# Cross-attention and expert kernel: the first loads and weight turns reordered, the mask spread by a product

## The chip, the cores and the metric

The kernel runs on one core of one Trainium2 chip, as one launch. The metric is device time in microseconds (us) of one execution; lower is better. A core has TensorE (PE: products and weight loads), VectorE (DVE), ScalarE (ACT), GpSimd (POOL) and SyncE (SP, which only issues transfers here). Each works through its own instructions in order and waits for the others by semaphores. SBUF is the on-chip memory, PSUM the memory that PE writes to.

## What is computed

Two layers on x (8 batches of 256 rows by 512 columns), each added to x after a layer norm.

1. Cross-attention. The rows of a batch (256) are channels, the 512 columns are positions. 16 heads of 16 channels:

```
q = Wq @ layernorm(x) + bq;  k = Wk @ src + bk;  v = Wv @ src + bv
mask = m[t] * m[s]
dot = mask * (q . k) / 4 - (1 - mask) * 1e6
out = (softmax(dot) * mask) @ v
x = x + out
```

2. A feed-forward layer on tokens (the 256 rows of each batch, 512 wide): a shared gated expert, a router that picks two of eight experts for each token, and the bf16 experts, weighted by the router's softmax.

The change touches only how the first batch's attention begins.

## The kernel before, in words

**Tiling.** Everything is laid out in tiles of 128 partitions. Attention works in groups of four heads: a batch has four groups (NG), the whole run 32, and `G` counts them. For each group, q and k tiles (128 x 512) hold four heads of 16 channels in blocks of 32 rows; the other 16 rows of a block carry mask and bias terms, so that one 32-row product yields the masked score. The rows come from `project_qk` (L393): a product with the turned weight (`product`, L399), then `rows` (L405), which on DVE multiplies the product by a 0/1 column (`mine`) and adds an extra tile. The extra tile is made by `extra_rows` (L380) from the mask spread over all partitions (`mb`) and the columns `alpha` and `beta`; `alpha` takes in the biases (`bias_terms`, L217).

**The loop over scores.** `row_max` (L419) computes scores of one quarter of the positions for two heads (two products into the PSUM banks s1 or s2), and DVE takes the row maximum into `nm`; eight calls make a group. `take_max` (L432) turns the maxima on PE (psn) and subtracts them from q on DVE. `exp_scores` (L441) computes the scores again the other way round, ACT takes the exponential, and `attend` (L455) multiplies with V, which `project_v` (L355) makes a quarter at a time. In the main loop (L1167 to L1244) the maxima run a group ahead of the exponentials.

**How order is set.** The order is written by hand (`manual_schedule`): program order is each engine's order. Fixed lists, such as `plan`, put the feed-forward work, the weight turns and the transfers at steps of the loop. The scheduler only adds the waits. Tiles come from pools with a number of buffers ("acc" has five, "e" three, PSUM's "mm" two); a new tile waits until the tile that many earlier is done with. Transfers of SP and ACT use eight semaphores in turn, so every ninth transfer waits until the eighth before it has landed.

**The start, which the change is about.** L126 to L136 issue the loads of batch 0: SP takes x's first half, the mask broadcast to 128 partitions (`partition_broadcast`, L128), x's second half, both halves of the context in one transfer, then Wv; ACT takes Wk, Wq and the two biases (`bflat`). `make_identity` (L139) makes `ident`. `row_terms` (L199) makes the 0/1 columns on DVE. Then come L1074 to L1103:
- `busy(n)` (L1042) issues n transposes of `ident` into a tile that nobody reads: filler on PE.
- `square` (L1049) turns a weight with four transposes (`turn_square`, L235; rows pt L239) and copies it out on ACT in four parts.
- `start_stats` (L341) takes mean and variance of half of x (DVE: st L327, mv L328, ve L330; POOL: rs L332).
- `shifted` (L1063) subtracts the mean and multiplies by the mask on DVE; `scaled` (L1070) multiplies by 1/sigma on ACT (first half), L1088 does so on DVE (second half).
- `mask_context` (L336) multiplies the context by the mask on DVE, two instructions.
- products `q_part`, `k_part` and rows `q_rows`, `k_rows` by parts.

Then eight `row_max` of group 0 (L1129 to L1141), with the turns of the shared expert's first weights between them (`weights`, pt L267), the mask columns `mcol`, and the router's load and turn (`load_router`, L248); k's rows for the second group (G = 1) come after the first maximum. `best = row_max(1, 0, 0, ...)`, `take_max(0)` and V's first quarter (L1146) follow, then the main loop.

Of the kernel before, what the change touches and what calls it, by code (L numbers as in the profile page):

```python
# [9 lines left out]
F32 = mybir.dt.float32  # L10
# [7 lines left out]
P = 128  # L18
# [8 lines left out]
NG = 4  # L27
# [9 lines left out]
def xattn_ffn_kernel(  # L37
# [85 lines left out]
        "mb": one.tile([P, T], F32, tag="mb", name="mb0"),  # L123
        "ctx": one.tile([P, 2, T], F32, tag="ctx", name="ctx0"),
    }
    nc.sync.dma_start(out=S[0]["x"][:, 0, :], in_=x[0, :P, :])  # L126
    wk_nat, wq_nat = load_square(Wk), load_square(Wq)
    nc.sync.dma_start(out=S[0]["mb"], in_=mask[0, 0].partition_broadcast(P))  # L128
    nc.sync.dma_start(out=S[0]["x"][:, 1, :], in_=x[0, P:, :])
    bflat = five.tile([2 * NG, 4, HD], F32, tag="acc", name="bflat")  # L130
    for side, bias in enumerate((bq, bk)):
        nc.scalar.dma_start(
            out=bflat[NG * side : NG * side + NG], in_=bias.rearrange("(c j d) -> c j d", j=4, d=HD)
        )
    nc.sync.dma_start(out=S[0]["ctx"], in_=src[0].rearrange("(h p) t -> p h t", p=P))
    wv_nat = load_square(Wv, nc.sync)  # L136

    ident = const.tile([P, P], F32, name="ident")
    make_identity(nc, ident)  # L139
# [77 lines left out]
    def bias_terms():  # L217

        for a in range(2):
            nc.vector.tensor_scalar(bnat[:, :, a, :], bflat, odd[: 2 * NG, a : a + 1], None, ALU.mult)  # L220
        pt = ps_m.tile([P, 2, NG // 2, 2], F32, tag="long", name="pt", bufs=1)
        nc.tensor.transpose(
            pt.rearrange("p s c a -> p (s c a)"), bnat.rearrange("r j a d -> r (j a d)"), ident[: 2 * NG, : 2 * NG]
        )
        of = lambda side: pt[:, side].rearrange("p c a -> p a c")
        nc.vector.scalar_tensor_tensor(alpha[:, 0], of(0), 0.25, terms[:, 0], ALU.mult, ALU.add)
        nc.vector.tensor_add(alpha[:, 1], of(1), terms[:, 1])

# [16 lines left out]
    sguT = wts.tile([P, 2, NKC, I + E], F32, name="sguT")  # L245
    sdT = wts.tile([P, 3, T], F32, name="sdT")

    def load_router():  # L248
        nat = five.tile([E, T], F32, tag="acc", name="wnat")
        nc.sync.dma_start(out=nat, in_=router_w)  # L250
# [90 lines left out]
    def start_stats(b, i):  # L341
        s = S[b]
        s["stats", i] = norm_stats(s["x"][:, i, :])
# [695 lines left out]
        assert not items  # L1039


    def busy(n):  # L1042

        for _ in range(n):
            nc.tensor.transpose(idle, ident, ident)

    idle = ps_av.tile([P, P], F32, tag="av", name="idle")

# [22 lines left out]
        nc.scalar.mul(s0["xm"][:, i, :], s0["xm"][:, i, :], s0["stats", i][1])  # L1071

    row_terms()
    busy(15)  # L1074
    square(wk_nat, WkT, 1.0, ps_s, "s1")
    busy(3)
    start_stats(0, 0)
    shifted(0)
    start_stats(0, 1)
    square(wq_nat, WqT, 0.25, ps_s, "s2")  # L1080
    bias_terms()
    busy(6)
    scaled(0)
    shifted(1)
    q_part, q_rows = project_qk(0, 0, True)
    k_part, k_rows = project_qk(0, 1, True)
    q_part(0)
    nc.vector.tensor_scalar(s0["xm"][:, 1, :], s0["xm"][:, 1, :], s0["stats", 1][1], None, ALU.mult)  # L1088
    extra_rows(0, 0, nc.scalar, (0,))
    mask_context(0, nc.vector)  # L1090
    busy(4)
    q_part(1)
    wv = turn_square(wv_nat, ps_s, "s2")
    extra_rows(0, 1, nc.scalar, (0,))
    q_rows(0)
    for kc in range(2):
        k_part(kc)
    k_rows(0)
    busy(8)
    nc.scalar.copy(WvT, wv)  # L1100
    extra_rows(0, 0, nc.scalar, (1,))
    extra_rows(0, 1, nc.scalar, (1,))
    q_rows(1)  # L1103
    for nm in NM:
        nc.gpsimd.memset(nm, 0.0)
    for e in range(E):
# [22 lines left out]
    for r in range(8):  # L1129
        row_max(0, r // 2, r % 2, ("s1", "s2")[r % 2])  # L1130
        if r % 2:
            weights.pop(0)[1]()
        else:
            busy(1 if r else 0)
        if r == 0:
            k_rows(1)
            pt = ps_m.tile([P, B * 4], F32, tag="long", name="pt", bufs=1)
            nc.tensor.transpose(pt, mnat, ident[: B * 4, : B * 4])
            nc.scalar.copy(mcol, pt)
        elif r == 1:  # L1140
            load_router()  # L1141
    best = row_max(1, 0, 0, "s1", True)
    busy(2)
    take_max(0)
    best()
    project_v(0, 0)  # L1146
    casts, turns = expert_weights()
    V_AT = [(2, 5), (2, 7), (3, 1), (3, 3)]
    blank = three.tile([P, T], BF16, tag="xnb", name="blank")
# [17 lines left out]
    for b in range(B):  # L1167
# [26 lines left out]
        for g in range(NG):  # L1194
            G = NG * b + g
            for h in range(8):
                st, half = divmod(h, 2)

                short = G == 0 and h < 6
                R = 8 * (G + 1) + h + LEAD - short  # L1200
                if (G or h) and R // 8 < last:
                    row_max(R // 8, (R % 8) // 2, R % 2)
                exp_scores(G, st, half if short else 1 - half, "s2" if R // 8 < last else ("s1", "s2")[h % 2])
                if G == 0 and h == 0:
                    row_max(1, 0, 1)
                if half == 0 and st > 0:
                    attend(G, st - 1)
                if G > 0 and h == 0:
                    attend(G - 1, NSTEP - 1)
                    divide_copy(G - 1)  # L1210
                if h == 8 - LEAD and G + 1 < last:
                    take_max(G + 1)
                if G > 0:
                    pb, pg = divmod(G - 1, NG)
                    if h == 1 + pg % 2:
                        divide(G - 1)
                    if pg % 2 == 1:

                        if b == pb == B - 1 and h == 5:
                            token_norm(pb, 0, nc.vector)  # L1220
                        elif h + (b == pb == B - 1) in FFN:
                            FFN[h + (b == pb == B - 1)](pb, pg // 2)
                if g == 0 and h == 6 and b + 1 < B:
                    load_batch(b + 1)
                if g == 1 and h == 0 and b + 1 < B:
                    mask_context(b + 1)
                if g == 1 and h in (2, 3) and b + 1 < B:
                    start_stats(b + 1, h - 2)
                if g == 1 and h == 5 and b + 1 < B:
                    start_norm(b + 1, nc.gpsimd)  # L1230
                if b == 0 and g == 0 and h in (0, 5, 7):
                    project_v(0, (0, 5, 7).index(h) + 1)
                if (g, h) in V_AT and b + 1 < B:
                    project_v(b + 1, V_AT.index((g, h)))
                if g % 2 == 1 and h == 7 and G + 3 < last:
                    extra_rows(G + 3, 0, nc.gpsimd)
                if g % 2 == 0 and h == 1 and G + 2 < last:
                    extra_rows(G + 2, 1, nc.gpsimd)
                if g % 2 == 0 and h in (1, 3) and G + 2 < last:
                    project_qk(G + 2, h // 2)  # L1240
                for go in plan[8 * g + h]:
# [88 lines left out]
```

## Time and profile before

| what | value |
|---|---|
| median of the runs | 871.96 us (870.93 to 879.49, three runs) |
| the profiled execution's own time | 873.27 us |
| its span (first to last instruction) | 871.5 us |
| mean granted clock of TensorE | 0.996 |
| busy: PE, DVE, ACT, POOL | 825.3, 581.8, 364.6, 312.2 us |
| instructions | 13399 |
| bytes moved by the transfers | 75.31 MB, 86 GB/s on average |

The profile is one execution, recorded in the same form for all engines. The page gives busy times and shares; the chain of waits is followed back from the last instruction, each step to what released it; the timeline lists instructions in order of time (start, length, engine, line, operation, out<-in, shapes, count; in brackets the idle time before and what ended it); the windows give the busy time of each engine in a stretch, with the clock granted to PE (1.00 is full speed) and the transfers' share and rate. Names such as `psq<-xm,WqT` are the program's own: the q product from the normalized x and the turned weight. One fp32 product of 512 columns shows as two records. "PEld" is PE's weight load, "SPq" and "ACTq" the issue of transfers.

### The profile page before, as it was taken

How to read it: one execution, taken by the hardware profiler on the slowest of the kernel's cores; microseconds unless marked ns; L12 is line 12 of the kernel's file. 1: busy time of each engine (PE TensorE's matmuls, PEld its weight loads, DVE VectorE, ACT ScalarE, POOL GpSimd, SP SyncE). 2: the span in 40 equal slices, each digit the busy share in tenths (PEclk: the TensorE clock that was granted, in tenths of full speed). 3: DMA queues.
4: the chain of work that ended last, by engine and by line, in shares of the span. 5: the costliest groups of instructions: out<-in, count | busy, mean ns of one | idle time of the engine just before them, and what ended most of it. 6: DMA issues, size and time to landing. Idle time of an engine off the chain costs nothing.

```text
span 871.5 us, 13399 instructions
## 1 busy us (share of the span) xinstructions
PE 825.3 (95%) x4978; PEld 341.4 (39%) x4990; DVE 581.8 (67%) x1105; ACT 364.6 (42%) x475; POOL 312.2 (36%) x380
## 2 busy tenths in 40 slices
PE   7988989999999999999999999999999999899997
PEld 5322333333333334333434333433343333455573
DVE  5766767775777676867786768676776674543347
ACT  3234444443444344433444343434343445356632
POOL 3114303542354345343625151605251223155520
PEclk8999999999999999999999999999999999999999
DMA  5116963221561157114712350001000000267646
GB/s 153 58 39 214 342 213 77 34 42 43 125 104 23 36 126 129 22 38 113 125 34 42 87 102 1 25 21 65 1 25 13 13 13 25 61 146 171 148 151 258
DMA packets 92099, 75.31 MB, mean 86 GB/s; under 512 B 60320, under 2 KB 77755, under 8 KB 91652
## 3 DMA queue, kind: packets, MB, share of 16 engines
q1 hardware_dynamic: 85428, 54.10, 23.1%
q0 software_dynamic: 5904, 19.70, 10.6%
q8 instruction: 40, 0.66, 0.4%
q10 hardware_dynamic: 704, 0.66, 0.2%
q14 instruction: 23, 0.19, 0.1%
HBM read 38.10 MB, written 40.79 MB: 91 GB/s over the span
## 4 chain that ended last, share of the span: by engine, by line
PE 70%; DVE 20%; issue 5%; POOL 2%; DMA 2%; ACT 1%; DVEq 0%; SPq 0%; POOLq 0%; ACTq 0%
PE s L425 24%; DVE nm L427 10%; PE av L463 9%; PE psy L987 5%; PE psq L400 4%; PE pu L929 3%; PE psk L400 3%; PE ey L838 2%; PE s L448 2%; DVE q L407 2%; PE eg L809 2%; PE psv L367 2%; PE eu L809 2%; PE pgu L929 2%; PE pg L929 2%
## 5 line engine op out<-in xcount | busy, mean ns | idle before, releaser
L450 ACT ACTIVATE e<-s 128x1024 f32<-128x1024 f32 x256 | 262.0, 1023 | 399.6 <-PE s L448 397.6
L427 DVE TENSOR_REDUCE nm<-s 128x2 f32<-128x1024 f32 x256 | 313.2, 1224 | 143.8 <-PE s L448 132.4
L425 PE MATMUL s<-k,q 32*128 32x512 f32 x1024 | 287.6, 640 | 26.5 <-DVE nm L427 24.4
L448 PE MATMUL s<-q,k 32*128 32x512 f32 x1024 | 288.5, 640 | 0.7 <-issue 0.7
L463 PE MATMUL av<-e,V 128*32 128x512 f32 x1024 | 137.4, 605 | 0.2 <-ACT e L450 0.2
L425 PEld LDWEIGHTS s<-k,q 32*128 32x128 f32 x1024 | 76.5, 183 | 131.8 <-DVE nm L427 108.0
L390 POOL TENSOR_SCALAR extra<-mb,alpha,beta 128x512 f32<-128x512 f32 x60 | 45.6, 764 | 147.0 <-DVE q L407 146.3
L332 POOL TENSOR_TENSOR rs<-ve,mhalf 128x1 f32<-128x1 f32 x32 | 17.9, 561 | 216.7 <-DVE ve L330 214.5
L448 PEld LDWEIGHTS s<-q,k 32*128 32x128 f32 x1024 | 76.5, 182 | 4.7 <-issue 4.3
L463 PEld LDWEIGHTS av<-e,V 128*32 128x32 f32 x1024 | 20.3, 108 | 98.2 <-issue 96.3
L187 POOL DMA_INDIRECT xs<-xnb,at x30 | 30.2, 1006 | 74.0 <-DVE at L658 59.3
L815 DVE SCALAR_TENSOR_TENSOR hz<-eth,eu 128x352 bf16<-128x352 f32 x45 | 23.4, 520 | 41.6 <-ACT eth L814 17.0
L987 PE MATMUL psy<-sdT,h 128*128 128x512 f32 (+1 forms) x90 | 45.3, 615 | 0.2 <-issue 0.2
L929 PE MATMUL pu<-xT,sguT 128*128 128x256 f32 x128 | 36.7, 403 | 0.0
L929 PE MATMUL pg<-xT,sguT 128*128 128x256 f32 x128 | 35.3, 401 | 0.0
L367 PE MATMUL psv<-WvT,ctx 128*128 128x256 f32 x128 | 34.7, 393 | 0.0
L929 PE MATMUL pgu<-xT,sguT 128*96 128x256 f32 (+1 forms) x128 | 34.1, 393 | 0.0
L809 PEld LDWEIGHTS <-late_ctx 128*128 128x128 bf16 x296 | 27.6, 98 | 14.0 <-issue 2.6
L400 PE MATMUL psq<-xm,WqT 128*128 128x512 f32 x64 | 33.0, 636 | 0.0
L187 POOL DMA_INDIRECT whose<-who,at x30 | 29.0, 968 | 9.1 <-issue 9.1
L407 DVE SCALAR_TENSOR_TENSOR q<-psq,mine,extra 128x512 f32<-128x512 f32 x32 | 22.6, 746 | 13.9 <-PE psq L400 13.9
L929 PEld LDWEIGHTS pu<-xT,sguT 128*128 128x128 f32 x128 | 21.8, 189 | 25.4 <-issue 23.6
(213 smaller groups left out, 987.5 us busy)
## 6 DMA issues: line engine op xcount, KB each, us to landing
xs<-blank SPq DMA_DIRECT2D x7, 1920.0 KB
ctx<-in_ctx_dram SPq DMA_DIRECT2D x8, 512.0 KB
x<-in_x_dram SPq DMA_DIRECT2D x7, 512.0 KB
accd<-acc SPq DMA_DIRECT2D x12, 256.0 KB
again<-accd POOLq DMA_DIRECT2D x12, 256.0 KB
out_dram<-again SPq DMA_DIRECT2D x12, 256.0 KB
gu<-in_L_ffn_w_gate_dram POOLq DMA_DIRECT2D x8, 352.0 KB
gu<-in_L_ffn_w_up_dram POOLq DMA_DIRECT2D x8, 352.0 KB
```

The source lines that it names most:

```text
L187: i = nc.gpsimd.indirect_dma_start(to[:, :], bass.IndirectOffsetOnAxis(ap=rows, axis=0), what, None, **bounds).ins
L367: nc.tensor.matmul(ps, ct[:, kc, sc * P : (sc + 1) * P], WvT[:, kc, :], start=(kc == 0), stop=(kc == 1))
L390: engine.tensor_scalar(t, S[b]["mb"], at, be, ALU.mult, ALU.add)
L400: nc.tensor.matmul(ps, W[:, kc, g // 2].rearrange("p j a d -> p (j a d)"), rhs[:, kc, :], start=(kc == 0), stop=(kc == 1),)
L425: nc.tensor.matmul(ps[:, jj, :], q[r, tci * P : (tci + 1) * P], k[r, :], start=True, stop=True)
L427: best = lambda: nc.vector.reduce_max(NM[G % 2][:, tci, c0 : c0 + 33 : 32], ps, axis=AX.X)
L448: nc.tensor.matmul(ps[:, jj, :], k[r, sc * P : (sc + 1) * P], q[r, :], start=True, stop=True)
L450: nc.scalar.activation(e, ps, AF.Exp)
L463: nc.tensor.matmul(AVT[G][32 * j : 32 * j + 32, :], V[:, sc, 2 * g + j // 2, j % 2 : j % 2 + 2, :].rearrange("p o d -> p (o d)"), et[j // ...
L809: nc.tensor.matmul(ps, xT[:, kc, :], weights_of(t, GU, I, (m * NKC + kc) * I), start=(kc == 0), stop=(kc == NKC - 1),)
L929: lambda kc=kc: nc.tensor.matmul(ps, sguT[:, m, kc, i0 : i0 + n + more], s["xT"][:, kc, :], start=(kc == 0), stop=(kc == NKC - 1))
L987: nc.tensor.matmul(t["y"], t["h"][:n, ic, tt * P : (tt + 1) * P], sdT[:n, ic, :], start=(ic == 0 and b < B - 1), stop=(ic == 2),)
```

## The change

Only the start and one step of the first group differ.

- Loads. SP issues x's two halves one after the other, then a single row of the mask (2 KB, into `mrow`, the rest of which a DVE memset has set to zero), then the context in two transfers, Wv and the router's weight. ACT issues the two biases first, then Wq, then Wk. `bflat`, `mrow` and the router's tile lie in the pool "e" instead of "acc".
- Mask. A constant `top` (128 x 128, ones in the first row, zero elsewhere; two memsets on DVE) is multiplied with `mrow` on PE: every partition of the product holds the mask row. ACT copies it to `mb`.
- Biases. The two multiplications of `bias_terms` go from DVE to ACT and stand first there; the turn on PE comes right after nine fillers (in place of fifteen). The DVE part is returned as `spread_out` and placed after the first statistics.
- Order. Wq is turned before Wk; first group's extra rows, the mask of the context and the second half's scaling come before the projections; Wv's turn comes after the k products instead of between the q and k products. The fillers are 9, 2, 3, 6, 2 and 5 in place of 15, 3, 6, 4 and 8.
- First maxima. k's rows of the second group come ahead of the first maximum; V's first quarter stands behind the third maximum's products instead of behind `take_max(0)`; the router is turned at r = 5 and its load has moved to the start; the fillers in that stage are two at r = 4 and r = 6 in place of one at r = 2, 4 and 6.
- Main loop. At G = 0, h = 5, three fillers (into a tile of the bank "long") follow the last maximum of group 1.

```diff
-    nc.sync.dma_start(out=S[0]["x"][:, 0, :], in_=x[0, :P, :])
-    wk_nat, wq_nat = load_square(Wk), load_square(Wq)
-    nc.sync.dma_start(out=S[0]["mb"], in_=mask[0, 0].partition_broadcast(P))
-    nc.sync.dma_start(out=S[0]["x"][:, 1, :], in_=x[0, P:, :])
-    bflat = five.tile([2 * NG, 4, HD], F32, tag="acc", name="bflat")
+    mrow = three.tile([P, T], F32, tag="e", name="mrow")
+    bflat = three.tile([2 * NG, 4, HD], F32, tag="e", name="bflat")
+    rnat = three.tile([E, T], F32, tag="e", name="rnat")
+    nc.vector.memset(mrow, 0.0)
+    top = const.tile([P, P], F32, name="top")
+    nc.vector.memset(top, 0.0)
+    nc.vector.memset(top[:1, :], 1.0)
+    for i in range(2):
+        nc.sync.dma_start(out=S[0]["x"][:, i, :], in_=x[0, i * P : i * P + P, :])
+    nc.sync.dma_start(out=mrow[:1, :], in_=mask[0])
     for side, bias in enumerate((bq, bk)):
         nc.scalar.dma_start(...)
-    nc.sync.dma_start(out=S[0]["ctx"], in_=src[0].rearrange("(h p) t -> p h t", p=P))
+    wq_nat, wk_nat = load_square(Wq), load_square(Wk)
+    for i in range(2):
+        nc.sync.dma_start(out=S[0]["ctx"][:, i, :], in_=src[0, i * P : i * P + P, :])
     wv_nat = load_square(Wv, nc.sync)
+    nc.sync.dma_start(out=rnat, in_=router_w)
...
-            nc.vector.tensor_scalar(bnat[:, :, a, :], bflat, odd[: 2 * NG, a : a + 1], None, ALU.mult)
+            nc.scalar.mul(bnat[:, :, a, :], bflat, odd[: 2 * NG, a : a + 1])
...
     row_terms()
-    busy(15)
-    square(wk_nat, WkT, 1.0, ps_s, "s1")
-    busy(3)
+    busy(9)
+    spread_out = bias_terms()
+    ps = ps_m.tile([P, T], F32, tag="mm", name="psm")
+    nc.tensor.matmul(ps, top, mrow, start=True, stop=True)
+    nc.scalar.copy(s0["mb"], ps)
     start_stats(0, 0)
+    spread_out()
     shifted(0)
+    extra_rows(0, 0, nc.scalar, (0,))
+    busy(2)
+    square(wq_nat, WqT, 0.25, ps_s, "s2")
     start_stats(0, 1)
-    square(wq_nat, WqT, 0.25, ps_s, "s2")
-    bias_terms()
-    busy(6)
     scaled(0)
     shifted(1)
+    busy(3)
+    square(wk_nat, WkT, 1.0, ps_s, "s1")
+    extra_rows(0, 1, nc.scalar, (0,))
+    busy(6)
+    nc.vector.tensor_scalar(s0["xm"][:, 1, :], s0["xm"][:, 1, :], s0["stats", 1][1], None, ALU.mult)
+    mask_context(0, nc.vector)
     q_part, q_rows = project_qk(0, 0, True)
     k_part, k_rows = project_qk(0, 1, True)
     q_part(0)
-    nc.vector.tensor_scalar(s0["xm"][:, 1, :], s0["xm"][:, 1, :], s0["stats", 1][1], None, ALU.mult)
-    extra_rows(0, 0, nc.scalar, (0,))
-    mask_context(0, nc.vector)
-    busy(4)
+    busy(2)
     q_part(1)
-    wv = turn_square(wv_nat, ps_s, "s2")
-    extra_rows(0, 1, nc.scalar, (0,))
     q_rows(0)
     for kc in range(2):
         k_part(kc)
     k_rows(0)
-    busy(8)
-    nc.scalar.copy(WvT, wv)
     extra_rows(0, 0, nc.scalar, (1,))
     extra_rows(0, 1, nc.scalar, (1,))
+    wv = turn_square(wv_nat, ps_s, "s2")
+    busy(5)
+    nc.scalar.copy(WvT, wv)
     q_rows(1)
+    k_rows(1)
...
-            busy(1 if r else 0)
+            busy(2 if r > 2 else 0)
         if r == 0:
-            k_rows(1)
...
-        elif r == 1:
-            load_router()
+        elif r == 2:
+            project_v(0, 0)
+        elif r == 5:
+            turn_router()
...
-    project_v(0, 0)
...
                 if G == 0 and h == 5:
                     row_max(1, 3, 1)
+                    busy(3, ps_m.tile([P, P], F32, tag="long", name="idle", bufs=1))
```

More of the change, by code (lines that the diff above doesn't have):

```diff
@@ L224, in bias_terms, with spread_out @@
         )
-        of = lambda side: pt[:, side].rearrange("p c a -> p a c")
-        nc.vector.scalar_tensor_tensor(alpha[:, 0], of(0), 0.25, terms[:, 0], ALU.mult, ALU.add)
-        nc.vector.tensor_add(alpha[:, 1], of(1), terms[:, 1])
+        def spread_out():
+            of = lambda side: pt[:, side].rearrange("p c a -> p a c")
+            nc.vector.scalar_tensor_tensor(alpha[:, 0], of(0), 0.25, terms[:, 0], ALU.mult, ALU.add)
+            nc.vector.tensor_add(alpha[:, 1], of(1), terms[:, 1])
+        return spread_out
     WqT = wts.tile([P, 2, 2, 4, 2, HD], F32, name="WqT")
@@ L246, in xattn_ffn_kernel, with turn_router @@
     sdT = wts.tile([P, 3, T], F32, name="sdT")
-    def load_router():
-        nat = five.tile([E, T], F32, tag="acc", name="wnat")
-        nc.sync.dma_start(out=nat, in_=router_w)
+    def turn_router():
+        nat = rnat
         pt = ps_m.tile([P, NKC, E], F32, tag="mm", name="pt")
@@ L1039, in spread, with busy @@
         assert not items
-    def busy(n):
+    def busy(n, into=None):
         for _ in range(n):
-            nc.tensor.transpose(idle, ident, ident)
+            nc.tensor.transpose(into or idle, ident, ident)
     idle = ps_av.tile([P, P], F32, tag="av", name="idle")
```

## The prediction

> **What bounds the kernel now.** I read the page's span and chain shares first, then the chain of waits over the first 34 us, then the timeline and the windows of that stretch, because the diff ends at about 53 us: all later code is word for word the same.
>
> ```profile
> span 871.5 us, 13399 instructions
> ...
> PE 70%; DVE 20%; issue 5%; POOL 2%; DMA 2%; ACT 1%; DVEq 0%; SPq 0%; POOLq 0%; ACTq 0%
> ```
>
> TensorE (PE) and VectorE (DVE) hold 90% of the chain. The steady loop hands over between them, the start does not. The chain of waits at the start (start, length, what):
>
> ```profile
> 1.64 6.84 DMA x<-in_x_dram
> 8.48 0.02 issue
> 8.51 0.71 DVE st L327
> ...
> 9.54 0.42 DVE bnat L220 x2
> 9.96 0.04 issue
> 10.00 0.27 PE pt L222
> 10.27 1.47 PE idle L1045 x6
> 11.75 1.71 PE psq L400 x2
> 13.45 0.85 PE idle L1045 x4
> 14.31 1.11 PE psq L400 x2
> 15.42 0.44 PE pt L239 x4
> 15.86 1.72 PE psk L400 x4
> 17.58 0.87 PE idle L1045 x8
> 18.45 0.04 issue
> 18.49 1.19 PE s L425 x7
> ```
>
> Until 8.48 the end is set by the load of x's second half; then by the bias turn, filler and projections on PE. The first score product starts at **18.49**. The same chain reaches the turn of the first maxima (psn) at 32.19, so the stage of eight maxima takes 13.70. Why are the projections so slow? The windows (length, busy PE, PEld, DVE, ACT, POOL, then granted clock, DMA share, GB/s) and the timeline say:
>
> ```profile
> 7.00:8.00 1.00, 0.13 (x1) 0.13 (x2) 0.75 (x1) 0.00 (x0) 0.00 (x0) 0.94 1.05 404
> 8.00:9.00 1.00, 0.99 (x4) 0.58 (x4) 0.49 (x1) 0.00 (x0) 0.00 (x0) 0.50 0.98 355
> ```
>
> ```profile
> 1.35 3.35 PE L1045 MATMUL idle<-ident 128*128 128x128 f32 x15 [1.35 <-POOL mhalf L154]
> ...
> 2.68 1.28 ACT L1056 ACT_TABLE_LOAD   x1 [2.68 <-issue]
> ...
> 7.08 0.75 DVE L1066 SCALAR_TENSOR_TENSOR xm<-x,mv,mb 128x512 f32<-128x512 f32 x1 [2.00 <-DMA mb<-in_mask_Bx1x_fk_dram]
> ```
>
> PE starved from 5.64 to 7.87, the granted clock fell to 0.50 at about 7.87 and came back between 14.6 and 14.7. One projection product costs 1.71 at half clock, 0.86 at full (psk: two in 1.72). Filler transposes cost 0.21 to 0.22 at half clock (six in 1.47), 0.11 at full (eight in 0.87). The fifteen of the opening also run at 0.22 (3.35/15): PE starts at half speed, although the windows print 1.00 there.
>
> **The change, part by part.** I build the new start on the same clock.
>
> Loads. The broadcast mask (256 KB written, landed 7.06) goes; a row of 2 KB comes. SP issues x0, x1 (0.73 to 1.6), then the mask row, which waits for a DVE memset; DVE is free from about 0.7 and POOL's 128x512 memset took 0.50, so it is done by 1.3 and holds up nothing queued behind it on SP. In before some 650 KB had landed by 4.6 (the windows' GB/s summed). x0, x1 and Wq are 768 KB, so they and the row queued behind x1 land at **about 5.0**, against 8.48 for x1. Wk and ctx follow by about 7, ahead of their use. SP's later issues: ctx1 waits for x0, Wv for a bias, the router's load moves ahead of mnat, bvb and gate rows, each at 0.34 to 0.6; all are used after 12, so they cost nothing. Gate rows and Wv no longer queue behind bflat and the router for the five "acc" buffers.
>
> Mask by product. On the path now: bias loads, table load, two bias multiplications on ACT, bias turn, product, ACT copy, all in order. Biases are issued first on ACT, at 0.7 to 1.65. Nearest row: the router's 16 KB load, issued at 19.69, released SP about 1.5 later (SP's waits). For the second bias, issued from 1.4, that gives 2.9; the Trainium skill (page DMA: Bandwidth & Descriptors, Anatomy of one DMA) puts the fixed cost of a transfer at some 2.0, which gives an estimate of 3.4. The row is the shorter and is this chip's; x's packets are in the way here: I take 3.0. The table load now waits for the biases: 3.0 to 4.3 (1.28). Multiplications: the same two took 0.42 on DVE, so 4.75; bias turn 0.27. The mask product is then ready at **5.1**, set equally by its row. It is one 128x512 product, 0.86 or 1.71.
>
> Clock. The Trainium skill (page TensorE: Matmul & The Clock Gate, Part 1) says that the throttle is lifted only after a busy window of about 3.4 us, free-running. This speaks against the change: nine fillers end at 3.35, then PE waits 1.4 for the biases. The row agrees in kind: in before, a gap of 1.02 (8.98 to 10.0) postponed the release to 14.67. By the rule the product is slow (1.71) and release comes between 8.5 and 11.9, after an unbroken 3.4 to 6.8 from 5.1; by the printed 1.00 it would be full speed throughout. I take half clock to 9.9.
> - Product 5.1 to 6.8, ACT copy (0.58, the row of WvT's copy) to **7.45**. No gain for the mask itself, which landed at 7.06.
> - DVE from there: shift 0.75, second statistics 1.10 (8.51 to 9.60), shift 0.75, scale 0.49, context mask 1.47: ends 12.0. In before it ended at 13.2, since x1 came late.
> - ACT: extra row 0.80, WqT copies 0.79 (Wq is turned by 8.1), scaled 0.74: xm's first half at 9.8.
> - PE: two fillers, Wq turn, three fillers, Wk turn, six fillers: 6.8 + 0.44 + 0.88 + 0.65 + 0.88 = 9.65; six fillers across the release, to 10.5. This is what the first q product waits for (ACT was ready at 9.8).
> - q product, two fillers, q product, two k products at full clock: 0.86 + 0.22 + 0.86 + 1.72, with 0.1 of gaps to 14.25; k rows on DVE 0.75: first score product at **15.0**, 3.5 earlier. Wv's turn and five fillers (0.99) lie beside the k rows.
> Both bounds: product at full clock at once, mask at 6.6, score at 13.4; release not before 11.9, score at 15.9.
>
> Stage of eight maxima. k of the second group moves ahead of the first maximum: +0.67 on DVE, but PE feeds that stage: two score products, the mask turn and four weight turns take 2.9 before the third score, and DVE ends the first maximum at 0.7 + 0.7 + 1.2 = 2.6. It removes the wait of the router's turn for those rows (1.35 of PE wait in before). From third score to psn, before: seven scores of 1.06, five fillers 1.15, three weight turns 1.66 = 10.2. After: 7.42 + V's first quarter 0.86 + six fillers 1.11 + 1.66 + router turn 0.25 = 11.3. So 2.9 + 11.3 = 14.2 against 13.70: **a loss of 0.5**. V left psn's other side, where its 0.86 lay beside DVE's subtraction (0.69): 0.07 saved there, and its 0.60 on DVE lay ahead of an 0.80 wait: nothing.
>
> Three fillers at the sixth step: in before PE waits 1.33 there (52.2 to 53.5) for a maximum; they take 0.33 to 0.6. If that cover were gone they would cost 0.33. The two DVE memsets for top (about 0.3) delay the mask terms, done at 3.1 while x0 lands at 3.96: cover 0.8.
>
> **Sum**: -3.5 + 0.5 = **-3.0**. The later loop is unchanged and every transfer in it is issued by program position, so the shift carries to the end. The profiled execution: 871.5 span plus 1.8 around it = 873.27; after, 868.5 span. It stands 1.3 above the median, 871.96; I carry the difference over: **869.0**.
>
> **Rivals.**
> 1. The main one: half clock through the mask product, release near 10: 869.0, own range 867.5 to 870.5. For: fillers of 0.22 in the opening. Chance 0.65.
> 2. PE at full speed from the mask product on. For: the printed 1.00, and two thirds of a busy window. Against: 0.22 per filler. Score at 13.4, saving 5.1 - 0.5 = 4.6: 867.4; with the biases and row also earlier by a microsecond, 866.2. Chance 0.15.
> 3. It doesn't do what it says: the earlier score is absorbed later, because a wait in the first batch (its buffers, loads of weights) was set by the old load times. Against: from 34 us on every piece of the chain is PE or DVE. Time 871.5 to 872.5. Chance 0.10.
> 4. Slower: the path of the biases. Everything now hangs on 1 KB loads that before had until 9.5 to land. If they or the row, sharing engines with x0 and Wq, release the mask product only at 8.1 instead of 5.1, the 3.0 are used up, and each microsecond later costs one. At 10: 873.9. For: the trace does not show when they landed. Against: 1.5 for the router. Chance 0.10.
>
> **How the numbers follow.** The likeliest is rival 1's 869.0. The range takes it, most of 2 and the near half of 3: 866.2 to 871.9, leaving 0.2 outside (deepest of 2, far half of 3, all of 4). One per cent, about what a measurement of this kernel tells from no change, is 8.7 us: no case reaches it except a mechanism I do not see in a start of 18.5 us. Faster by over 1%: 0.03; within: 0.93; slower: 0.04.
>
> **What would show it.** The first score product (18.49) near 15.0; the mask copy ending near 7.45; the second statistics following the first shift with no wait for x; the q products each near 0.86 and the granted clock 1.00 there; the psn turn 14.2 after the first score; the table load beginning near 3.0. Wrong if the mask product begins after 6, if the clock is 0.50 in the score stage, or if the difference at 60 us is not the difference at the end.

## The result, and the profile after

Times are the slowest core's; the changed kernel and the kernel before ran in turn on the same chips, 20 executions each.

| | before | after |
|---|---|---|
| median (lowest to highest), us | 877.51 (870.93 to 882.70) | 870.64 (868.61 to 872.55) |
| the profiled execution, its span | 873.27, 871.5 | 869.63, 867.8 |
| mean granted clock in the profile | 0.996 | 1.000 |

The ratio of after to before is 0.9943, 95% interval [0.9921, 0.9966]: 0.6% faster. (Ratios, here and below, leave out the three executions that lie more than 1.5% above the fastest of their kernel: two of v_only, one of the kernel before.) The forecast was 869.0 from 871.96, a saving of 3.0; the medians differ by 6.9, the means by 5.1. The change did less in the profile's start than forecast, and much more elsewhere, because 871.96 was not the time of the kernel before. Its executions fall in two groups with nothing between: of these 20, nine lie at 870.9 to 872.6 (mean 871.4) and eleven at 877.4 to 882.7 (mean 879.3). The later runs of it, 207 with a clock reported for each, show the same gap: 120 with a median of 872.8 at a mean clock of 0.995 or more, 87 with 879.4 at 0.990 or less. The two groups are the main finding here, so below each kernel is given with the number of its executions at 0.990 or less ("low"; the rest are "not low"). Of the changed kernel, none of 42 is there; its lowest mean clock is 0.995. That 870.6 lies near the forecast 869.0 is partly luck: against the executions of before that are not low (871.4) the change saves 0.8, and the rest of the gain comes from a group that the forecast did not know.

The page of the changed kernel (span, then shares of the chain that ended last, by engine):

```profile
span 867.8 us, 13410 instructions
...
PE 74%; DVE 19%; issue 3%; POOL 2%; ACT 1%; DMA 0%; DVEq 0%; ACTq 0%; POOLq 0%
```

DMA has left the chain (2% before). Its chain of waits through the start and the first maxima (start, length, what):

```profile
1.31 1.97 DMA bflat<-in_L_xattn_bk_dram
...
3.38 1.28 ACT L228
...
5.58 2.02 PE psm L1088 x2
...
8.24 0.75 DVE xm L1077
...
12.62 1.12 PE psq L411 x2
13.75 1.73 PE psk L411 x4
...
30.44 0.45 PE psn L447 x4
```

The order of events is the forecast one: bias, table load, multiplications, bias turn, mask product, copy, shift. The first score product starts at 16.38 (18.49 before), the turn of the maxima at 30.44 (32.19). So 2.11 us are gained at the start and 0.36 given back in the stage of eight maxima (14.06 long, 13.70 before). The clock was released at 8.96 and stayed at 1.00 to the end, where before it was 0.50 from 7.87 to 14.70.

Behind 32 us the two profiles keep a distance of about 1.76 until 240 us. It then grows twice, by some 0.8 at 254 and at 434 us, to 3.66 in the span. The timelines of before and after at the first place:

```profile
253.28 0.97 DVE L587 TENSOR_TENSOR w<-w,m 128x16 f32<-128x16 f32 x1
253.44 1.51 POOL L390 TENSOR_SCALAR extra<-mb,alpha,beta 128x512 f32<-128x512 f32 x2
```

```profile
251.40 0.18 DVE L598 TENSOR_TENSOR w<-w,m 128x16 f32<-128x16 f32 x1
...
251.56 1.51 POOL L401 TENSOR_SCALAR extra<-mb,alpha,beta 128x512 f32<-128x512 f32 x2
```

The same 16-column product takes 0.97 or 0.18. In both profiles POOL's 128x512 `extra` (0.76 each) starts 0.16 after DVE's product has begun; in the long case DVE's ends 0.06 after POOL's first. Another profile of the same kernel before (b_same) has neither delay. Over the 20 profiles of these experiments the two instructions meet in this way at three places each (near 250, 340 and 430 us). DVE's took 0.93 or more in 12 of the 60, always with POOL starting 0.15 or 0.16 behind it; at the same distance it was short more often than long. So it falls differently in executions of one kernel, and why DVE is held at all by an instruction that starts after its own the traces don't show. The 1.76 is then what the profiles show of the change itself.

### The profile page after: what moved, and what is told of

Read it like the earlier page. It is cut to its first block, busy times and chain, and to the rows that moved or that the text cites. A ratio compares the mean times of both kernels' runs of the same rounds, so it can differ in the third digit from the quotient of the medians.

```text
span 867.8 us, 13410 instructions
## 1 busy us (share of the span) xinstructions
PE 826.3 (95%) x4987; PEld 340.0 (39%) x4987; DVE 580.8 (67%) x1106; ACT 365.6 (42%) x478; POOL 312.6 (36%) x380
## 4 chain that ended last, share of the span: by engine, by line
PE 74%; DVE 19%; issue 3%; POOL 2%; ACT 1%; DMA 0%; DVEq 0%; ACTq 0%; POOLq 0%
PE s L436 24%; DVE nm L438 10%; PE av L474 9%; PE psy L998 5%; PE pu L940 4%; PE psq L411 3%; PE psk L411 3%; PE ey L849 3%; PE eu L820 3%; PE eg L820 3%; PE pgu L940 3%; PE pg L940 3%; DVE q L418 2%; PE s L459 2%; PE psv L378 2%
## 5 line engine op out<-in xcount | busy, mean ns | idle before, releaser
L411 PE MATMUL psk<-ctx,WkT 128*128 128x512 f32 x64 | 31.6, 617 | 0.0
```

Of the source, the lines that this page charges most:

```text
L411: nc.tensor.matmul(ps, W[:, kc, g // 2].rearrange("p j a d -> p (j a d)"), rhs[:, kc, :], start=(kc == 0), stop=(kc == 1),)
```

## The experiments

Two theories stood after the result. *The start*: the earlier scores and nothing else make the gain, and the rest is a draw. *The clock* (D in the expectations that use letters): PE loses its clock in the first 60 us of many executions of the kernel before, in a wait that the change fills or removes. The recorded expectations name further ones by letters and say what each is: A (collisions of DVE and POOL), B (the start), C (the end of the kernel), E (the busy share of PE alone). In the table, "this" is the kernel's median, "low" the number of its executions at a mean clock of 0.990 or less; the ratio is to the kernel before on the same chip.

| kernel | this, us (n) | ratio [95%] | low |
|---|---|---|---|
| b_same | 878.34 (14) | 1.0021 [0.9983, 1.0060] | 8 |
| start_only | 877.70 (14) | 1.0003 [0.9969, 1.0038] | 10 |
| maxima_only | 874.33 (22) | 0.9988 [0.9965, 1.0011] | 0 |
| a_nofill | 872.38 (22) | 0.9972 [0.9952, 0.9992] | 0 |
| fill128 | 873.13 (14) | 0.9975 [0.9941, 1.0010] | 5 |
| fill32 | 872.90 (22) | 0.9978 [0.9954, 1.0003] | 5 |
| a_same | 871.39 (22) | 0.9957 [0.9935, 0.9979] | 0 |
| nm_early | 870.40 (22) | 0.9952 [0.9935, 0.9969] | 0 |
| k_only | 873.59 (12) | 0.9969 [0.9934, 1.0004] | 3 |
| v_only | 875.95 (12) | 0.9989 [0.9951, 1.0028] | 2 |
| third128 | 874.21 (13) | 0.9978 [0.9949, 1.0007] | 1 |
| third32 | 880.89 (12) | 1.0020 [0.9980, 1.0059] | 8 |
| kv_only | 874.37 (12) | 0.9995 [0.9967, 1.0023] | 0 |
| best | 870.53 (12) | 0.9962 [0.9942, 0.9982] | 0 |
| both128 | 873.72 (12) | 0.9986 [0.9959, 1.0013] | 0 |
| both32 | 879.28 (12) | 1.0006 [0.9972, 1.0040] | 7 |

The kernel before had 19 low of 59 beside the first four rows, 31 of 67 beside the next four, 17 of 35 beside k_only to third32, 7 of 23 beside kv_only and best, 13 of 23 beside the last two. The medians of its executions that are not low were 872.9, 872.4, 873.6, 872.8 and 872.1, so times of different sets differ by up to 1.5 us with no change of the kernel. A median of it, or of a kernel like it, jumps by 6 us with which side of one half the low share falls on; counts say more here than medians.

### Which part: the start or the maxima

b_same is the kernel before itself. start_only is the changed kernel with the maxima of before and without the three fillers of the main loop:

```diff
-    k_rows(1)
...
-            busy(2 if r > 2 else 0)
+            busy(1 if r else 0)
         if r == 0:
+            k_rows(1)
...
-        elif r == 2:
-            project_v(0, 0)
-        elif r == 5:
+        elif r == 1:
             turn_router()
...
+    project_v(0, 0)
...
-                    busy(3, ps_m.tile([P, P], F32, tag="long", name="idle", bufs=1))
```

> The kernel before, unchanged, to see what differs between its own executions: its 20 times fall into two clusters, nine near 871 us and eleven from 877 to 883. Theory A (a shared port: short two-input DVE instructions wait for a POOL instruction that works beside them, a race decided anew in each batch): an execution near 878 shows seven to ten such waits of 0.4 to 1.6 us in the routing stage (w<-w,m took 0.97 and 0.93 instead of 0.18 in the profile), spread over the batches, and a start like the profiled one. Theory B (the start: the broadcast of the mask or a longer half clock): the whole difference of 7 us lies ahead of 35 us. Theory C (the end, from 750 us on, where transfers work at 150 to 260 GB/s): the difference lies there.

> Only the start of the change (loads, mask product, biases, turns, fillers up to the first score product); the stage of eight maxima and the main loop as before. First score product at 16.4 as in the changed kernel. If the maxima part costs the 0.36 us that the two traces show between first score and psn (2.11 earlier at the first score, 1.75 at psn), psn stands at 30.1 here. Theory B: the upper cluster is gone, since the broadcast and the half clock are gone; times 868.5 to 872. Theory A: the clusters depend on where the DVE and POOL work of the later batches meets, which the start doesn't set, so the upper cluster may be there or not.

maxima_only is the kernel before with the other half of the change (the router is still loaded and turned at r = 1):

```diff
+    k_rows(1)
...
-            busy(1 if r else 0)
+            busy(2 if r > 2 else 0)
         if r == 0:
-            k_rows(1)
...
+        elif r == 2:
+            project_v(0, 0)
...
-    project_v(0, 0)
```

> Only the stage of the first maxima (k of the second group ahead, V's first quarter at the third step, two fillers at r = 4 and 6); start as before, router loaded and turned at r = 1. First score product at 18.5, psn within 0.5 us of the 32.2 of before, so by itself worth nothing: 870.5 to 872 in the lower cluster. Theory B: the upper cluster near 878 remains. If the upper cluster is gone here, the cause lies in the first maxima or V.

a_nofill is the changed kernel without the last line of its diff, the three fillers at G = 0, h = 5.

> The changed kernel without the three fillers in the main loop (first group, step 5). They lie in a wait of DVE of 0.85 to 1.33 us, so nothing at that place: within 0.3 us of the changed kernel, 870.6. If the fillers are what ended the upper cluster (by keeping PE's clock up), it is back here.

**Measured.** The start alone does not lower the median (877.70): 10 of 14 executions are low. In its other four the median is 870.6, against 872.9 in those executions of before beside it that are not low: there the 2.1 us of the profile come through. maxima_only is the reverse: no low execution, but its 874.3 is 1.5 above those 872.9. The count hides something there: seven of its 22 lie at 0.991 or 0.992 and average 876.4, the other fifteen, at 0.995 or more, 873.6. Its profile is one of the seven (877.07 us, clock 0.50 from 36.09 to 42.92), so a stretch of 7 us at half clock is left, where start_only's profile has one of 17. a_nofill has no low ones either; its 872.4 misses the 870.6 that was expected, on another chip than a_same's 871.4, and whether the loop's fillers are worth the difference stays open. So the long losses go with the maxima stage, the earlier scores with the start, and the loop's fillers are not needed to end the low group.

start_only's profile is a low execution. Its windows (length, busy PE, PEld, DVE, ACT, POOL, then clock, DMA share, GB/s):

```profile
17.64:21.05 3.41, 2.14 (x13) 0.98 (x13) 3.06 (x4) 0.77 (x2) 0.00 (x0) 1.00 0.39 136
21.05:38.12 17.07, 17.07 (x46) 6.93 (x43) 7.33 (x7) 1.65 (x3) 2.56 (x4) 0.50 0.13 42
```

Its first score came 2.6 ahead of before's profile, yet the stretch that follows ran at half clock, and the span is 877.6. In those 17 us PE counts as busy without a break, and the clock comes back only at their end. The Trainium skill (page TensorE: Matmul & The Clock Gate, Part 1) says that one busy window of about 3.4 us lifts the throttle. The length agrees: granted clocks change here at whole multiples of 3.413 us from each other (4.46, 7.87, 14.70 in the profile of before). The condition does not: the first four of these five busy windows lifted nothing. What PE runs there is mostly score products of 32 rows, a quarter of the array's 128.

Theory A can be settled from the traces. both32's profile is a low execution (879.20 us) with none of the long products of the section on the result, the profile of before (873.27) has two and v_only's (875.51) three: these collisions do not make the low group.

### Is it the wait for the router's turn, and do busy time or rows count?

PE waits 1.35 us for k's rows ahead of the router's turn (timeline of before):

```profile
21.67 0.35 PE L253 MATMUL pt<-ident,wnat 8*128 8x8 f32 x3 [1.35 <-DVE k L407]
```

fill128 puts four filler products there, fill32 the same on 32 rows (1.06 and 1.15 us of PE):

```diff
         elif r == 1:
+            for _ in range(4):
+                nc.tensor.matmul(idle, ident[:128, :], ident[:128, :], start=True, stop=True)
             load_router()
```

> The kernel before with four filler products of 128 rows by 128 columns put ahead of the router's load and turn (r = 1), where PE waits 1.35 us for k's rows of the second group. Theory D (the upper cluster is the clock: a window of about 3.4 us around 18 to 21.5 us, in which PE's rows are little used, drops the clock to half, and the score products, which use 32 of 128 rows, cannot lift it again for up to 17 us): the window gets 0.8 us more of full rows, so the upper cluster (mean clock 0.990 or less, 57% of one set of runs of before, 32% of another) is gone or nearly so; times 871 to 874. Theory E (busy share alone decides): the same. Theory A (port collisions): the upper cluster stays.

> The same four filler products at the same place on 32 of the 128 rows: PE's busy share in the window rises by the same amount, the rows used by a quarter of it. Theory D: the upper cluster stays, a third to a half of the runs near 878 to 880 with mean clock 0.990 or less. Theory E: it is gone, as with 128 rows.

**Measured.** 5 low of 14 and 5 of 22: this wait alone is not the cause, and no difference by rows shows here. One detail was of use later: the deepest low executions (mean clock 0.983 and below), of which b_same had two in 14 and the runs of before beside these five in 67, are in neither; what is left lies at 0.987 to 0.990. At that rate about three would be expected in 36, so their absence is a hint and no more.

a_same is the changed kernel itself, and nm_early is it with POOL's two memsets of the maxima tiles moved behind the first statistics:

```diff
     start_stats(0, 0)
+    for nm in NM:
+        nc.gpsimd.memset(nm, 0.0)
...
-    for nm in NM:
-        nc.gpsimd.memset(nm, 0.0)
```

> The changed kernel itself, beside the others on one chip. Theory D: no run with a mean clock of 0.990 or less; median 870 to 872.

> The changed kernel with the two POOL memsets of the maxima tiles (0.98 us) moved from behind the second 1/sigma to behind the first, where POOL waits for 4.6 us. In the changed kernel the scaling of xm's second half took 1.46 us beside them instead of 0.49. If the two collide at a shared port, the scaling takes about 0.5 here, the second q product starts 0.9 earlier, the first score product at 15.4 to 15.5 instead of 16.38, and the time falls by 0.9: ratio to the changed kernel 0.999. If the 1.46 has another cause, nothing moves.

In the changed kernel these memsets meet DVE's scaling of x's second half, on the path; the timelines of after (POOL, DVE, PE), of before (DVE) and of nm_early (DVE):

```profile
11.03 0.98 POOL L1122 MEMSET nm<- 128x512 f32 x2
11.11 1.46 DVE L1103 TENSOR_SCALAR xm<-xm,rs 128x512 f32<-128x512 f32 x1 [0.45 <-POOL rs L343]
...
12.62 1.12 PE L411 MATMUL psq<-xm,WqT 128*128 128x512 f32 x2 [0.90 <-DVE xm L1103]
```

```profile
11.31 0.49 DVE L1088 TENSOR_SCALAR xm<-xm,rs 128x512 f32<-128x512 f32 x1
```

```profile
10.88 0.52 DVE L1105 TENSOR_SCALAR xm<-xm,rs 128x512 f32<-128x512 f32 x1 [0.45 <-POOL rs L343]
```

In after, PE's second q product waited 0.90 for that scaling. Its 1.46 became 0.52 in nm_early, whose first score starts at 15.22. The page SBUF — State Buffer of the Trainium skill (SBUF: two separate sides) says that DVE and POOL share a pair of ports, which, for some of DVE's operations, the first of the two holds for its whole instruction; that fits, since DVE ended 0.56 after POOL's second memset. The median is 1.0 us lower than a_same's, though the ratios' intervals overlap.

### Halves of the maxima stage

k_only moves `k_rows(1)` ahead of the first maximum, v_only moves `project_v(0, 0)` to r = 2, each in the kernel before; kv_only does both. The fillers stay as in before.

```diff
+    k_rows(1)
...
         if r == 0:
-            k_rows(1)
```

```diff
+        elif r == 2:
+            project_v(0, 0)
...
-    project_v(0, 0)
```

> The kernel before with one edit: k's rows of the second group ahead of the first maximum. It takes away PE's wait of 1.35 us at the router's turn, so the third score product comes about 0.7 us earlier. If that wait is what drops the clock, no run has a mean clock of 0.990 or less and the times are 871 to 874. If the clock falls for want of 128-row work in the whole stage of maxima, a third to a half of the runs remain near 878 to 880.

> The kernel before with one edit: V's first quarter (two products of 128 rows, 0.86 us) moved from behind the turn of the maxima to the third step of the stage. If 128-row work inside the stage is what keeps or restores the clock, no run at 0.990 or less; if the wait ahead of the third score product decides, a third to a half remain.

> The kernel before with both moves of the maxima stage, k's rows ahead of the first maximum and V's first quarter at the third step, but its own fillers (one at r = 2, 4, 6). If the two moves together end the long stretches of half clock, no run at a mean clock of 0.990 or less, as in maxima_only (none of 22) and unlike k_only (3 of 12) and v_only (2 of 12). If the second filler at r = 4 and 6 is needed, one in six or more remain.

**Measured.** 3 of 12, 2 of 12, and with both none of 12. Each move lowers the count at best in part, as far as a dozen executions can tell (v_only's two are the deepest of all, 0.979 at 887.0 and 888.5 us). With both the low group is gone, as in maxima_only's 22, without the second filler and without the new start. Five of kv_only's twelve lie at 0.991 or 0.992: short losses of clock (one window at 54.1 us in its profile) remain.

third128 and third32 leave the order of before alone and put the four fillers at the third step (1.06 and 1.15 us), where V's quarter goes in the change:

```diff
+        elif r == 2:
+            for _ in range(4):
+                nc.tensor.matmul(idle, ident[:128, :], ident[:128, :], start=True, stop=True)
```

> The kernel before with four filler products of 128 rows (eight records, 1.06 us at full clock) at the third step, where the changed kernel has V's products. They cost about 1 us in a stage that PE bounds: 873 to 874 at full clock. If 128-row work in the stage decides, no run with a mean clock of 0.990 or less.

> The same fillers at the third step on 32 of 128 rows: as long on PE (1.15 us for the eight records), a quarter of the rows. If rows count, a third to a half of the runs stay at a mean clock of 0.990 or less, near 879 to 881; if the busy share counts, they go as with 128 rows.

**Measured.** 1 of 13 against 8 of 12. The one that is left is the profiled execution of third128 (885.27 us), with a mean clock of 0.983: its clock drops at 23.04, before the fillers, which come at 24.5. That suggests two places: the wait at the router's turn for the deepest losses, and the score products behind it for the others.

### Both places at once: the decisive pair

both128 and both32 are the kernel before with the fillers at r = 1 and r = 2, on 128 or 32 rows. Nothing is moved.

> The kernel before with both fillers of 128 rows: four in the wait for the router's turn and four at the third step. Reading of the earlier runs: the first removed the runs at a mean clock of 0.983 and 0.984 (none left of 14, as with 32 rows), the second those at 0.986 to 0.990 (none left of 13). Together they should leave none, or one, at 0.990 or less in a dozen, with nothing moved; the median 873.5 to 874.5, since the fillers of the third step lie on the path (1.06 us). If the two together leave three or more, the long stretches come from elsewhere.

> The same eight fillers on 32 rows: the same busy time, a quarter of the rows. If rows are what counts, three or more of a dozen stay at 0.986 to 0.990 (third32 had 8 of 12, fill32 5 of 22, before about 4 in 10), at 878 to 883 us. If busy time counts, none or one, as in both128.

**Measured.** None of 12, and 7 of 12, the first inside its expectation of 873.5 to 874.5 and the second as expected if rows count. Their profiles happen to have the same place of the clock's windows: one starts 3.0 us after the first score product in both. The windows of both128, then of both32:

```profile
21.54:24.95 3.41, 3.25 (x21) 1.88 (x21) 2.46 (x3) 0.19 (x1) 0.00 (x0) 1.00 0.42 127
24.95:42.00 17.05, 16.71 (x78) 6.87 (x76) 12.27 (x15) 3.70 (x5) 2.58 (x4) 1.00 0.14 42
```

```profile
21.27:24.68 3.41, 3.19 (x22) 1.66 (x22) 2.52 (x3) 0.19 (x1) 0.00 (x0) 1.00 0.48 134
24.68:41.74 17.06, 17.06 (x48) 7.38 (x46) 7.85 (x7) 1.65 (x3) 2.57 (x4) 0.50 0.13 42
```

PE is busy for 3.25 and 3.19 of 3.41 us, as good as equal. Weighted by the rows that each product uses, of 128, the same windows come to 0.47 and 0.27 of the array (worked out from the products' recorded times and rows). After the first the clock stays at 1.00, after the second it is 0.50 for 17 us, and PE gets through 48 records of products in place of 78. The fillers of the two kernels differ in their rows, and with these in the weights that they load and in how many ones of `ident` they multiply; which of these counts the pair does not tell apart, so "rows" stands for all three. The pair also shows that the effect does not need the change: full-row work put into the two places does the same for the low group. The fillers cost what they take: 873.7 is 1.6 above the 872.1 of before's executions beside it that are not low. In the changed kernel PE waits 0.61 at the first place and V's quarter stands at the second (timeline of after):

```profile
18.91 1.13 PE L436 MATMUL s<-k,q 32*128 32x512 f32 x4 [0.61 <-DVE nm L438]
19.96 1.13 PE L378 MATMUL psv<-WvT,ctx 128*128 128x256 f32 x4
```

The three windows of its profile from 15.8 to 26.0 us use 0.48, 0.58 and 0.41 of the array by the same working, where the window ahead of start_only's drop used 0.23.

### Where the kernel before loses it, and the best version

b_look and b_look2 are the kernel before, each for one more profile.

> The kernel before once more, for one profile. If its time is near 878 or above (one in two or three), the granted clock drops to 0.50 at 18 to 23 us or at 50 to 60 us, and the lost time lies in those stretches, the rest being as in the profile shown first. If it is near 872, only the stretch of half clock from about 8 to 15 us shows.

> A second draw of the profile of the kernel before, with the same expectation as the first: near 878 or above, the clock drops to 0.50 at 18 to 23 us or at 50 to 60 us and the lost time lies there; near 872, only the stretch of half clock from about 8 to 15 us shows.

The first took 872.13, the second 883.61 us. Windows of b_look, then of b_look2:

```profile
19.60:23.05 3.45, 2.10 (x21) 1.06 (x13) 2.81 (x4) 0.96 (x3) 0.00 (x0) 1.00 0.29 79
23.05:43.53 20.48, 19.50 (x97) 7.62 (x97) 15.44 (x18) 4.72 (x6) 3.35 (x5) 1.00 0.14 47
```

```profile
19.60:23.05 3.45, 2.10 (x19) 1.16 (x15) 2.81 (x4) 0.94 (x3) 0.00 (x0) 1.00 0.22 72
23.05:43.53 20.48, 20.48 (x53) 7.96 (x49) 9.22 (x9) 1.67 (x4) 2.57 (x4) 0.50 0.15 47
```

Up to 23 us the two do the same (2.10 busy). Then the second gets through 53 records of products where the first has 97; it loses one more window at 64.01. Against the profile shown with the prediction, b_look2 is 0.8 late at the first score, 9.5 at 43 us, 11.0 at 68 us and 10.3 at the end: the whole loss lies in the first 70 us. On the page, all that shows it is the row of granted clocks, whose second digit of forty is 5 in place of 9. This is the deeper and rarer kind of low execution: of the 87 low ones of the kernel before, 17 lie at 0.984 or less. Of the commoner kind, 0.985 to 0.990, there is no profile of the kernel before itself, only of start_only and both32.

Why does one execution lose it and the next not? Six profiles share the code up to there (before, b_same, b_look, b_look2, third32, third128). In four, a clock window begins up to 0.27 us after the first score product, or 0.4 before it; in the two that lose the clock, 0.38 and 0.43 after. The windows are not tied to the kernel's start (the first change of the clock comes between 4.20 and 6.30 us in the profiles with the start of before), so each execution draws where they fall. Six profiles suggest that the place matters. The use of the array doesn't tell them apart: the window ahead comes to 0.26 or 0.27 in b_same, b_look and third32, which keep the clock, and to 0.26 in the two that lose it. What decides between them stays open.

best is nm_early with six fillers behind the turn of the maxima, where PE waits 0.78 for the subtraction: three profiles of the changed kernel's family lost the clock just there (a_nofill at 33.84, a_same at 32.87, nm_early at 32.39).

```diff
     take_max(0)
+    busy(6)
```

> The changed kernel with the maxima tiles' memsets earlier (nm_early) and six fillers behind the turn of the maxima, in the 0.78 us in which PE waits for the subtraction. Two traces of the changed kernel and nm_early lost the clock for a window or two just there (29.0 to 32.9), at 0.33 and 0.36 of rows used. If 128-row work keeps the clock, the mean clock is 0.999 to 1.000 in nearly every run, and the median falls from 870.4 (nm_early) to 869.5 to 870.

The clock came out nearly as expected (0.998 to 1.000 in all twelve), the median did not: 870.53, with nm_early at 870.40. The two ran on different chips; against the executions of before beside them that are not low they are 2.3 and 2.0 lower. The lost windows do cost something: nm_early's seven executions at 1.000 average 870.0, its other fifteen 870.8. What the six fillers save there and what they cost themselves can't be told apart at this size. nm_early, best and the changed kernel itself all end the low group; between them these runs don't decide.

## Why the prediction was right or wrong, point by point

**The base failed.** "It stands 1.3 above the median, 871.96; I carry the difference over" took the median of three runs for the kernel's time. One of those three, 879.49, was an execution of the other group; it was in the table, and was passed over. With it read as a second kind of execution, the question would have been what the change does to that kind.

**The step that failed: "The later loop is unchanged and every transfer in it is issued by program position, so the shift carries to the end."** It carries in the profile, 1.76 us, but PE's clock does not go by program position. The clock was followed only to the first score product; the maxima stage was priced as a loss of 0.5, and that it sets the use of the array in the windows at 18 to 25 us was not seen. In its place the runs show this: of the mean difference of 5.1 us (875.75 to 870.63 over the 20 executions each), 0.55 x (879.3 - 871.4) = 4.3 is the group that is gone, and 0.8 the shift of the others. The shift itself falls short of the profile's 1.76 for the same reason. The changed kernel's eight executions at 0.999 or 1.000 average 869.8, 1.6 below 871.4; its other twelve, with short losses of clock, average 871.2.

**The first score product, 15.0: mis-sized, 16.38.** Term by term:
- Bias landing "I take 3.0": 3.28. The row taken, 1.5 from the router, was the worse neighbour; the 2.0 of the Trainium skill (page DMA: Bandwidth & Descriptors, Anatomy of one DMA), weighed there and not taken, agrees with the 1.97 measured (the section is about transfers that GpSimd issues, this one is ACT's). Multiplications 0.42: 0.59 on ACT. Mask product at 5.1: 5.58.
- Mask product 1.71: 2.02 until its end, at half clock as forecast. The copy ended at 8.21, not 7.45: 0.76 late.
- From there DVE and POOL were costed by their rows of before as if alone. `rs` took 1.00 instead of 0.57 beside DVE's shift, the second scaling 1.46 instead of 0.49 beside the memsets: 1.4 late, partly in slack. The second q product waited 0.90 for it; the forecast had PE as the limit there.
- Release "to 9.9", bounds 8.5 to 11.9: 8.96, inside. The products behind it ran at full clock: psk 1.73 for two, as forecast 1.72.
- The sum hides two errors that cancelled: the first q product began at 10.38, forecast 10.5, since the earlier release made up for the late copy. The 1.4 were lost behind it, 0.90 of them in the wait for the scaling.

**The stage of eight maxima, 14.2: right in the profile**, 14.06. As a loss of 0.5 it is 0.36 there; over many executions the stage costs about 1.5 (maxima_only, kv_only). About half of that goes with short losses of clock: maxima_only's fifteen executions at 0.995 or more average 873.6, 0.7 above the 872.9 of before.

**The fillers of the sixth step, "cover", cost nothing: right.** PE still waits behind them (timeline of after):

```profile
50.36 0.55 PE L1056 MATMUL idle<-ident 128*128 128x128 f32 x3
51.75 0.70 PE L436 MATMUL s<-k,q 32*128 32x512 f32 x2 [0.85 <-DVE nm L438]
```

**The rivals.** Full speed from the mask product on was wrong (2.02). The shift was not absorbed. The slower path of the biases is the right mechanism at a small size: 0.48 late, against the 3.0 from which it would have decided.

## What to carry to other kernels

When a few runs of a kernel differ by more than the rest agree, first find out what the odd ones are: a mean clock of 0.988 in place of 0.996 is some 7 us here, in a stretch of about 20 us. Look for PE's half-clock stretches not only where PE is idle but also where it runs products of few rows, and try work that uses all rows (useful work, such as V's projection, before filler) between them and into the wait ahead. An earlier start is only kept if what follows it keeps the clock.

## What the runs showed of the hardware that was not expected

- The granted clock goes with the rows in use better than with PE's busy share. Weighted by rows, the windows after which it dropped used 0.14 to 0.37 of the array, over the 13 drops between 21 and 64 us in eleven profiles; their busy share was 0.54 to 0.93, and PE's longest gap in them 0.22 to 1.35 us. Counted in the same way from 18 us on, the 20 profiles have some 4900 windows at full clock. Only 96 of them used 0.37 or less: those 13, and 83 that kept the clock, some as low as 0.15. Of the windows with a busy share of 0.93 or less more than a thousand kept it. So low use goes ahead of every drop but does not always bring one, and what exactly the gate counts stays open.
- At half clock it did not come back in windows that were busy throughout, at 0.34 to 0.71 of rows, and came back after windows of 0.46 to 0.95 (13 times). The same 32-row products kept it at 1.00 for as long where it was not lost.
- The row of granted clocks prints 1.00 in the opening although the fillers there take 0.22, twice their time later; it shows nothing of the clock ahead of its first change.
- A small operation of DVE (128x16) that takes 0.18 us in one execution takes 0.93 or more in another of the same kernel, with an instruction of POOL starting 0.15 or 0.16 us behind it in both.
